# A two-layer attention kernel: which engine scales and sums q's weight in the first sample, and where the last sample's reciprocal and statistics stand

## The chip, the cores and the metric

The kernel runs on one core of one Trainium2 chip. The metric is the device time of a whole run in microseconds (us), smaller is better. Beside the plain runs there is one profiled execution, from which all the views below are taken; its times count from the start of its span.

## The reference

Eight samples of 512 channels by 1024 positions, float32, go through two attention layers one after the other. Cut to what matters:

```python
# layer 0: group norm, 8 heads of 64
h = group_norm(x, norm_w, norm_b)
q, k, v = split(einsum('oc,bchw->bohw', qkv_w, h) + qkv_b)
o = softmax(q @ k.T / sqrt(64)) @ v
x = x + einsum('oc,bchw->bohw', proj_w, o) + proj_b
# layer 1: norm over a whole sample, one head of 512
n = (x - mean) * rsqrt(var + 1e-5) * gn_gamma + gn_beta
q = wq @ n + bq;  k = wk @ n + bk;  v = wv @ n + bv
out = x + wo @ (v @ softmax(q.T @ k / sqrt(512)).T) + bo
```

In layer 1 the kernel multiplies weights together first: one 512 by 512 weight, called `wqk1` (the product of wq and wk), replaces q's and k's, and one called `wvo1` (wv and wo) replaces v's and the output's. The gain gamma is multiplied into these products, into `wqk1` by rows and by columns.

## The kernel before

**Samples and stages.** The samples are worked through one after another. Each has, in order: V of layer 0, q and k of layer 0, the attention of layer 0, the projection of layer 0 (which, for all but the last sample, comes after the next sample's first q and k), then layer 1: q, V, scores, values. What is needed only once, the two weight products and the scaling by gamma, stands ahead of the first sample and partly in it.

**Products.** Every large product is made by a fast scheme with seven block products in place of eight (`strassen`, or `by_two_steps` with the scheme inside the scheme). TensorE adds up two of a group's four results in one PSUM bank, `line`, and two in another, `single`. ScalarE copies `line` away as u1, u2 and u3 as it goes, and VectorE adds `single` and the copies together (`done`, lines 712, 729, 1285). TensorE can write `single` again only after VectorE has read it, and `line` after ScalarE has. The scheme needs sums of the weight's blocks, S1 to S4: `finish` (L195) makes them with four VectorE operations of 128x512 elements for a whole weight, and `sums_a` (L511) makes those of the second level, sixteen operations of 128x128 for one `WeightTwice`. Made once, they are stored to DRAM and read back for later samples.

**Order.** The orders on TensorE, ScalarE and VectorE are those in which the program is written. `together` takes one step of each of several products in turn, and `at_steps(steps, hooks)` runs the functions of hooks[n] after step n. GpSimd (POOL) and SyncE (SP), which issues nearly all transfers, have queues of their own, in an order that a scheduler makes at build time; each of them starts its instructions in that order. Weights stand in three buffers; a load into a buffer waits for the last reader of the weight before.

**The first sample.** The stage `pairs_qk(w, 0, ...)` makes q and k of half the channels, with ten steps. Its hooks make `wvo1` ready, run `through_q` (which multiplies rows of `wqk1` by gamma on ScalarE, L236, and its columns by a row of gamma on GpSimd, L241, eight operations of 128x256), make the second-level sums of `wvo1` on VectorE (step 5), finish the weight of V, `v0`, at step 7 and `wqk1` at step 8, and at step 9 make the second-level sums of `qk02`. The second-level sums of `wqk1` go onto a list, `over`, which the next stage, V of the first sample, takes as hooks 0 to 3; they are issued to GpSimd. `rows_q` is a transfer of a small result to DRAM, and the eight transfers `c_q` (L774) read it back in single elements of four bytes.

**The last sample.** Its projection (L1263 on, `last` true) has to divide by a sum over keys that is not there yet when it starts: four matmuls (`add_keys`, L1024) make the sum in `spares[0]`, the second half of the tile that has the first product's `single`, VectorE takes its reciprocal (L860) and multiplies. `Ready.measure` runs the next of the list `due`, each entry two passes of ScalarE over half a chunk (L333), for layer 1's mean and variance. Part way through V of layer 1, VectorE makes sums of layer 1's query, `halve_a("S1")`, at step 13.

Of the kernel before, what the change touches and what calls it, by code (L numbers as in the profile page):

```python
# [39 lines left out]
ALU = mybir.AluOpType  # L40
# [6 lines left out]
P = 128  # L47
C = 512
# [17 lines left out]
def two_attention_blocks(  # L66
# [18 lines left out]
    nc = tc.nc  # L85
# [16 lines left out]
    def tile2(name):  # L102
        return tpool.tile([P, 2, HALF], FP, tag="t", name=name)

    def tile_u(name):
        return upool.tile([P, HALF], FP, tag="u", name=name)
# [93 lines left out]
    class Weight:  # L200
# [3 lines left out]
        def __init__(self, name):  # L204
            self.name, (self.src, self.widths) = name, SOURCES[name]
            self.tile = wpool.tile([P, W_SIZE], FP, tag="w", name=f"w_{name}")
            self.parts, self.rest, at = [], [], 0
            for width in self.widths:
                size = len(A_PARTS) * 2 * width
                self.parts.append(parts_of(self.tile[:, at : at + size], width))  # L210
                at += size
            if name in stored:
                nc.sync.dma_start(self.tile, stored[name])
# [24 lines left out]
        def scale_columns(self, row):  # L238
            for cc in range(NC):
                for to, a in self.moving(cc):  # L240
                    nc.gpsimd.tensor_tensor(a, a, row[:, to], ALU.mult)  # L241

        def finish(self):
            for parts, rest in zip(self.parts, self.rest):
# [43 lines left out]
    def room(name, n=-1):  # L288

        return spares[n] if spares else banks("s", f"ps_{name}")[:, 0, :]  # L290
# [207 lines left out]
    def sums_a(q, t, engine=nc.vector):  # L498

        t = t if len(t.shape) == 2 else flat(t)  # L500
        n = t.shape[1] // 4
        for i in range(4):
            part = t[:, i * n : (i + 1) * n]
            if len(q["A11"].shape) == 3:
                part = part.rearrange("p (u o) -> p u o", u=2)
            q[f"S{i + 1}"] = part
        for i, x, y, op in [
            (1, "A21", "A22", ALU.add), (2, "S1", "A11", ALU.subtract),
            (3, "A11", "A21", ALU.subtract), (4, "A12", "S2", ALU.subtract),
        ]:  # L510
            engine.tensor_tensor(q[f"S{i}"], q[x], q[y], op)  # L511
        return q
# [36 lines left out]
    class WeightTwice:  # L549

        def __init__(self, name, make=None, later=None):
            tiles = [flat(tile2(f"{name}_twice_{n}")) for n in range(2)]
            key, self.tiles = f"{name}_twice", tiles
            if make is None:

                nc.scalar.dma_start(tiles[0], stored[key][:, : 8 * P])
                nc.scalar.dma_start(tiles[1], stored[key][:, 8 * P :])
                return  # L560
            stored[key] = dram.tile([P, 16 * P], FP, tag=key, name=f"stored_{key}")

            def step(n, i, a):
                sums_a(
                    self.quarters(a, make), tiles[n][:, i * 4 * P : (i + 1) * 4 * P],
                    nc.vector if later is None else nc.gpsimd,
                )
                if i == 1:
                    nc.sync.dma_start(stored[key][:, n * 8 * P : (n + 1) * 8 * P], tiles[n])

            steps = [
                lambda n=n, i=i, a=a: step(n, i, a)
                for n, pair in enumerate(PAIRS) for i, (a, _) in enumerate(pair)
            ]
            if later is not None:
                later.extend(steps)
                return
            for now in steps:
                now()

        def quarters(self, a, rows_of):
            return {f"A{i + 1}{j + 1}": rows_of(i, a)[:, j, :] for i in range(2) for j in range(2)}
# [275 lines left out]
    def one_over(ps, name):  # L858
        inv = accpool.tile([P, HALF], FP, tag="inv", name=f"inv_{name}")[:, : ps.shape[1]]
        nc.vector.reciprocal(inv, ps)  # L860
        return inv
# [29 lines left out]
    def both_of(w):  # L891
        return lambda i, name: w.parts[i][name]
# [34 lines left out]
    def columns_of(w):  # L927
        return lambda i, name: w.parts[0][name][:, :, i * P : (i + 1) * P]
# [26 lines left out]
    def layer0(bs, qs, ks, b, norm_next):  # L955
# [5 lines left out]
        if norm_next is not None:  # L961
            for n in range(NC):
                hooks[n + 4] = [lambda cc=n, half=half: norm_next.of_half(cc, half) for half in range(2)]
            hooks[8] = [lambda cc=cc: norm_next.of_channels(cc) for cc in range(NC)]
        for n, step in enumerate(over):
            hooks.setdefault(n, []).append(step)
        over.clear()
        twice_b = {}
        if b > 0:
# [50 lines left out]
        def add_keys(pair, gs, ps):  # L1020

            n = P // 2 // len(gs)
            for i, (g, j) in enumerate((g, j) for g in gs for j in range(2)):
                nc.tensor.matmul(  # L1024
                    ps[i * n : (i + 1) * n, :], ones[:, :n], accs[pair, g][:, j, :],
                    start=True, stop=True,
                )
# [46 lines left out]
        def combine1():  # L1074
            nc.vector.tensor_tensor(comb["T1"], os[0][1], os[0][0], ALU.subtract)
# [187 lines left out]
        def project(w, c):  # L1263
            def done(i, half, bank, u):
                chunk = c + 2 * i
                x = piece(xs, chunk, half)

                def add():
                    nc.vector.scalar_tensor_tensor(  # L1269
                        x, bank if u is None else u, bias[:, chunk : chunk + 1], x, ALU.add, ALU.add  # L1270
                    )
                    due.append(lambda: norm.moments(chunk, half, i == half))
                    if (i, half, c) == (1, 0, 1):
                        ready.halve("B21")


                first = last and i == half == 0
                if first and c == 0:
                    ps_sum = spares[0]
                    add_keys(end, [1], ps_sum)  # L1280
                    combine1()
                    combine2(2, 0)
                    combine2(3, 0)
                if u is not None:
                    nc.vector.tensor_tensor(u, bank, u, ALU.add)
                if not first:
                    add()
                    return
                later.append(add)
                if c == 0:  # L1290
                    invs[end] = one_over(ps_sum, f"0_{b}_{end}_1")
                    divide(end, 1, invs[end])
                else:

                    held(flat(accs[end, 1]), f"acc_0_{b}_{end}", flat(accs[end, 1]))
                    for n, k in [(2, 1), (3, 1), (4, 0), (4, 1)]:
                        combine2(n, k)
                    for more in later:
                        more()

            return strassen(by_channels(w, c, comb), done, f"p_0_{b}_{c}")

        w = next_weight().parts[0]
        hooks = {} if last else {2 * n - 3: [lambda n=n: combine2(n, 1)] for n in range(2, 5)}
        for n, counts in [(1, 1), (2, 1), (7, 1), (8, 2), (9, 2)]:
            hooks.setdefault(n, []).append(lambda n=counts: ready.measure(n))
        hooks[2].append(ready.load)
        hooks[7].append(lambda: ready.halve("B22"))
        at_steps(together(project(w, 0), project(w, 1)), hooks)
        if last:  # L1310
# [3 lines left out]
    class Ready:  # L1314
# [9 lines left out]
                self.due.pop(0)()  # L1324

        def load(self):
            self.weights = WeightTwice("wqk1")

        def halve(self, name, engine=nc.gpsimd):
            self.quarters[name] = quarters_b(  # L1330
# [3 lines left out]
    def attention1(xs, norm, ready, b, at_values):  # L1334
# [19 lines left out]
        def halve_a(name, t=None, engine=nc.vector):  # L1354
            q = {f"A{n}": v for n, v in halve(q_parts[name], lambda i, j: (j, i)).items()}
            twice_a[name] = sums_a(q, flat(tile2(f"{name}_twice_{b}")) if t is None else t, engine)
# [115 lines left out]
        def finish_q(n):  # L1472
            q_parts[f"S{n}"] = tile2(f"s{n}_q_{b}")
            finish(q_parts, a21, n)

        at_steps(make_v_twice(w, twice_w[0], bs, twice_b, v_pairs, f"v_1_{b}"), {
            **{2 * n + 3: [lambda n=n: finish_q(n)] for n in range(1, 5)}, 13: [lambda: halve_a("S1")],
        })


# [375 lines left out]
        nc.tensor.matmul(ps[:, 0:1], ones, good, start=True, stop=True)  # L1856
        nc.vector.tensor_copy(flag, ps[0:1, 0:1])

    made, throughs, over, gamma_row = {}, [], [], []


    with tc.manual_schedule(engines={PE, ACT, DVE}):
# [31 lines left out]
                        nc.vector.tensor_tensor(t, t, vec[:, V_NW1 : V_NW1 + NC], ALU.mult)  # L1894

        def through_v():
            gamma_row.append(tile2("gamma_row")[:, 0, :])
            nc.sync.dma_start(gamma_row[0], gamma1.to_broadcast([P, C]))
            throughs.append(Through(wvo1, bias_v, wo1, "v", room("rows_v", 0)))
            wvo1.scale_rows(V_NW1, range(1))  # L1900

        def through_q():
            throughs.append(Through(wqk1, bias_q, nk1, "q", room("rows_q", 0)))
            wqk1.scale_rows(V_NW1)
            wqk1.scale_columns(gamma_row[0])

        def channels_of(half, ccs):
            for cc in ccs:
# [21 lines left out]
        at_steps(together(*pairs_qk(w, 0, combine.parts, qs, ks, 0)), {  # L1930
            1: [lambda: combine.make(2), wvo1.finish], 2: [through_q, lambda: combine.make(3)],
            4: [lambda: combine.make(4)], 5: [lambda: WeightTwice("wvo1", columns_of(wvo1))],
            7: [waiting[0].finish], 8: [wqk1.finish], 9: [
                lambda: WeightTwice("qk02", both_of(w)), lambda: WeightTwice("wqk1", columns_of(wqk1), over),
            ],
        })
        bs = combine.parts
        for rows in throughs:
# [434 lines left out]
```

## Time and profile before

| | us | what it is |
|---|---|---|
| Median of 3 runs | 2829.9 | 2828.9 to 2829.98 |
| The profiled execution | 2828.29 | whole run |
| Its span | 2825.7 | first to last instruction |
| PE busy | 2806.3 | 99% of the span, 19.4 us idle |
| DVE (VectorE) busy | 2114.7 | 75% |
| ACT (ScalarE) busy | 1171.2 | 41% |
| POOL (GpSimd) busy | 394.3 | 14% |

A busy share is an average over stages. PE stands still for 19.4 us of the span, and the view of waits says for whom. In a timeline each line gives the start, the length, the engine, the line of the program, the operation, what it writes from what it reads, how many are merged, and in brackets the idle time before it and who ended it. "SPq" is SyncE's queue, and the length there is the time that issuing the transfer took.

### The profile page before, as it was taken

How to read it: one execution, taken by the hardware profiler on the slowest of the kernel's cores; microseconds unless marked ns; L12 is line 12 of the kernel's file. 1: busy time of each engine (PE TensorE's matmuls, PEld its weight loads, DVE VectorE, ACT ScalarE, POOL GpSimd, SP SyncE). 2: the span in 40 equal slices, each digit the busy share in tenths (PEclk: the TensorE clock that was granted, in tenths of full speed). 3: DMA queues.
4: the chain of work that ended last, by engine and by line, in shares of the span. 5: the costliest groups of instructions: out<-in, count | busy, mean ns of one | idle time of the engine just before them, and what ended most of it. 6: DMA issues, size and time to landing. Idle time of an engine off the chain costs nothing.

```text
span 2825.7 us, 39407 instructions
## 1 busy us (share of the span) xinstructions
PE 2806.3 (99%) x15688; PEld 1585.4 (56%) x15688; DVE 2114.7 (75%) x2867; ACT 1171.2 (41%) x1760; POOL 394.3 (14%) x412
## 2 busy tenths in 40 slices
PE   9999999999999999999999999999999999999999
PEld 5434765357653576435764466734667346673375
DVE  6677697776967678676787767777777777767777
ACT  3364224643246332563325533255332643326622
POOL 2000220012200231002400024000240002400121
PEclk9999999999999999999999999999999999999999
DMA  7513132231313313233131331313313132121001
GB/s 264 203 46 122 58 111 85 70 113 53 126 64 87 105 53 112 68 91 109 70 106 45 91 124 56 108 49 87 121 57 108 50 114 93 64 95 48 23 16 39
DMA packets 83865, 247.50 MB, mean 88 GB/s; under 512 B 21817, under 2 KB 22617, under 8 KB 77273
## 3 DMA queue, kind: packets, MB, share of 16 engines
q1 hardware_dynamic: 73768, 209.75, 22.6%
q10 hardware_dynamic: 9904, 35.16, 3.8%
q8 instruction: 125, 2.05, 0.3%
q14 instruction: 68, 0.55, 0.1%
HBM read 188.02 MB, written 33.03 MB: 78 GB/s over the span
## 4 chain that ended last, share of the span: by engine, by line
PE 92%; DVE 6%; issue 1%; DMA 0%; ACT 0%; ACTq 0%; POOL 0%; DVEq 0%; POOLq 0%
PE s L992 16%; PE ps_o L1011 16%; PE ps_o L1686 7%; PE ps_v L695 7%; PE ps_p L680 6%; PE ps_l_qk L917 5%; PE ps_l L1522 4%; PE ps_s L1505 4%; PE ps_s_qk L910 4%; PE ps_l_q L680 3%; PE ps_l_v L695 3%; PE ps_s L1522 3%; PE ps_o_qk L910 3%; PE ps_s_v L938 2%; PE ps_s_q L1380 2%; PE ps_s_two L1816 2%
## 5 line engine op out<-in xcount | busy, mean ns | idle before, releaser
L846 ACT ACTIVATE p<-s 128x1024 f32<-128x1024 f32 x512 | 523.5, 1024 | 329.2 <-PE s L992 323.1
L848 DVE TENSOR_TENSOR acc<-acc,p 128x1024 f32<-128x1024 f32 x384 | 469.1, 1222 | 99.2 <-ACT p L846 90.3
L1011 PE MATMUL ps_o<-p,v 64*64 64x512 f32 x4096 | 528.7, 589 | 0.0
L992 PE MATMUL s<-c_q,c_k 64*64 64x512 f32 x3584 | 465.1, 590 | 0.0
L1011 PEld LDWEIGHTS ps_o<-p,v 64*64 64x64 f32 x4096 | 156.6, 133 | 282.8 <-issue 278.0
L992 PEld LDWEIGHTS s<-c_q,c_k 64*64 64x64 f32 x3584 | 134.7, 133 | 253.2 <-issue 236.1
L528 POOL TENSOR_TENSOR B_twice<-x 128x512 f32<-128x512 f32 x16 | 20.4, 1274 | 1353.8 <-DVE x L1269 1353.3
L1686 PE MATMUL ps_o<-t_p,s_v 128*128 128x512 f32 x384 | 168.2, 594 | 0.0
L848 DVE TENSOR_TENSOR acc<-p,p 128x1024 f32<-128x1024 f32 x64 | 78.2, 1222 | 79.7 <-ACT p L846 79.7
L1496 ACT ACTIVATE p<-p,factor 128x512 f32<-128x512 f32 (+1 forms) x112 | 85.3, 780 | 115.9 <-DVE p L1532 91.4
L1510 ACT COPY p<-ps_s 128x512 f32<-128x512 f32 x96 | 53.1, 588 | 176.6 <-PE ps_s L1505 176.6
L1686 PEld LDWEIGHTS ps_o<-t_p,s_v 128*128 128x128 f32 x384 | 72.3, 190 | 91.3 <-issue 89.2
L1532 DVE TENSOR_TENSOR p<-ps_l,p 128x512 f32<-128x512 f32 x136 | 89.8, 682 | 40.0 <-PE ps_l L1522 39.7
L459 ACT COPY u_v<-ps_v 128x512 f32<-128x512 f32 x48 | 28.1, 585 | 212.3 <-PE ps_v L695 193.4
L680 PE MATMUL ps_p<-t_p,w_p 128*128 128x512 f32 x256 | 112.8, 593 | 1.8 <-ACT u_p L459 1.2
L1532 DVE TENSOR_TENSOR p<-ps_s,p 128x512 f32<-128x512 f32 x112 | 74.8, 684 | 37.8 <-PE ps_s L1522 37.8
L695 PE MATMUL ps_v<-w_v,t_again 128*128 128x256 f32 x448 | 99.0, 379 | 0.0
L373 POOL TENSOR_TENSOR rstd<-rstd,minus_half 128x4 f32<-128x4 f32 (+1 forms) x16 | 12.8, 798 | 567.3 <-DVE rstd L372 567.3
L695 PEld LDWEIGHTS ps_v<-w_v,t_again 128*128 128x128 f32 x448 | 85.1, 190 | 11.6
L695 PE MATMUL ps_v<-w_v,x 128*128 128x256 f32 x384 | 87.3, 380 | 0.9 <-DVE q L712 0.9
L680 PE MATMUL ps_p<-o,w_p 128*128 128x512 f32 x192 | 86.9, 594 | 0.2 <-DVE o L1031 0.2
L680 PEld LDWEIGHTS ps_p<-t_p,w_p 128*128 128x128 f32 x256 | 48.5, 190 | 63.7 <-issue 59.1
(507 smaller groups left out, 5165.8 us busy)
## 6 DMA issues: line engine op xcount, KB each, us to landing
x<-in_x SPq DMA_DIRECT2D x92, 512.0 KB, 6.5
w_qk<-stored_qk SPq DMA_DIRECT2D x14, 1792.0 KB, 7.2
w_wqk<-stored_wqk SPq DMA_DIRECT2D x8, 1792.0 KB, 7.2
fold<-acc SPq DMA_DIRECT2D x56, 256.0 KB, 3.1
qk_twice<-stored_qk_twice ACTq DMA_DIRECT2D x28, 512.0 KB, 5.9
w_wvo<-stored_wvo SPq DMA_DIRECT2D x8, 1792.0 KB, 8.8
out<-x SPq DMA_DIRECT2D x28, 512.0 KB, 4.8
w_v<-stored_v SPq DMA_DIRECT2D x7, 1792.0 KB, 7.4
```

Of the source, the lines that this page charges most:

```text
L680: nc.tensor.matmul(bank, w[a][:, k, c * P : (c + 1) * P], bs[b][:, k, :], start=fresh and k == 0, stop=k == 1, skip_group_check=True,)
L695: nc.tensor.matmul(bank[:, u * 2 * P : (u + 1) * 2 * P], bs[b][:, k, n * P : (n + 1) * P], w[a][:, k, :], start=fresh and u == k == 0, sto ...
L846: nc.scalar.activation(p, s, AF.Exp, scale=factor)
L848: nc.vector.tensor_tensor(acc, first, p, ALU.add)
L910: nc.tensor.matmul(bank[:, i * 2 * P : (i + 1) * 2 * P], parts[a][x], twice_b[v][y], start=start and i == 0, stop=True, skip_group_check=True,
L917: nc.tensor.matmul(bank, of(i, a)[:, k, :], bs[v][:, k, :], start=start and k == 0, stop=k == 1, skip_group_check=True,)
L992: nc.tensor.matmul(s[cols, j, :], ks[pair][k0 // HALF][rows, k0 % HALF : k0 % HALF + HD], qs[pair][g][rows, :], start=True, stop=True,)
L1011: nc.tensor.matmul(o[cols, half, :], vs[kt][rows, c0 : c0 + HD], p[rows, j, :], start=kt == 0, stop=kt == NT - 1,)
L1505: nc.tensor.matmul(bank, bs[v][:, k, t * P : (t + 1) * P], q_parts[a][:, k, :], start=a == "A11" and k == 0, stop=k == 1, skip_group_check ...
L1522: nc.tensor.matmul(bank[:, u * 2 * P : (u + 1) * 2 * P], v[y][:, u * P : (u + 1) * P], a[x], start=start and u == 0, stop=True, skip_group ...
L1532: nc.vector.tensor_tensor(at(r, t), bank, at(r, t), ALU.add)
L1686: nc.tensor.matmul(bank, v_parts[kt // 2][a][:, kt % 2, c * P : (c + 1) * P], p_parts[kt // 2][b][:, kt % 2, cols], start=fresh and kt == ...
```

## The change

In the first sample the multiplication of `wqk1`'s columns by gamma goes from GpSimd to VectorE, out of `through_q` and into step 2 of V; `wqk1.finish` goes from step 8 of the stage before to step 3 of V; `v0`'s finish goes from step 7 to step 8, behind VectorE's add for q there. The second-level sums of `wqk1` go from GpSimd, in V, to VectorE, at step 5 of the first sample's projection, where the kernel before read them back from DRAM. The row of gamma is loaded after `rows_q` is stored and not before the first sample.

In the last sample ScalarE copies the sum over keys to a tile `total`, and the reciprocal reads that; the first two `measure` go from steps 1 and 2 to steps 5 and 6; `halve_a("S1")` goes from step 13 to 17.

```diff
@@ scale_columns
-                    nc.gpsimd.tensor_tensor(a, a, row[:, to], ALU.mult)
+                    nc.vector.tensor_tensor(a, a, row[:, to], ALU.mult)
@@ WeightTwice.__init__(self, name, make=None)
-            def step(n, i, a):
-                sums_a(
-                    self.quarters(a, make), tiles[n][:, i * 4 * P : (i + 1) * 4 * P],
-                    nc.vector if later is None else nc.gpsimd,
-                )
...
-            if later is not None:
-                later.extend(steps)
-                return
...
+            for n, pair in enumerate(PAIRS):
+                for i, (a, _) in enumerate(pair):
+                    sums_a(self.quarters(a, make), tiles[n][:, i * 4 * P : (i + 1) * 4 * P])
+            for n in range(2):
+                nc.sync.dma_start(stored[key][:, n * 8 * P : (n + 1) * 8 * P], tiles[n])
@@ layer0
-        for n, step in enumerate(over):
-            hooks.setdefault(n, []).append(step)
+        for n, step in over:
+            hooks.setdefault(n, []).insert(0, step)
@@ the projection
                 if first and c == 0:
-                    ps_sum = spares[0]
+                    ps_sum, total = spares[0], tile_u(f"total_0_{b}")
                     add_keys(end, [1], ps_sum)
+                    nc.scalar.copy(total, ps_sum)
...
-                    invs[end] = one_over(ps_sum, f"0_{b}_{end}_1")
+                    invs[end] = one_over(total, f"0_{b}_{end}_1")
...
-        for n, counts in [(1, 1), (2, 1), (7, 1), (8, 2), (9, 2)]:
+        for n, counts in [(5, 1), (6, 1)] if last else [(1, 1), (2, 1)]:
             hooks.setdefault(n, []).append(lambda n=counts: ready.measure(n))
-        hooks[2].append(ready.load)
+        for n, counts in [(7, 1), (8, 2), (9, 2)]:
+            hooks.setdefault(n, []).append(lambda n=counts: ready.measure(n))
+        hooks.setdefault(2 if b else 5, []).append(ready.load)
@@ Ready.load
-            self.weights = WeightTwice("wqk1")
+            self.weights = WeightTwice("wqk1", None if self.b else columns_of(waiting[0]))
@@ V of layer 1
-            **{2 * n + 3: [lambda n=n: finish_q(n)] for n in range(1, 5)}, 13: [lambda: halve_a("S1")],
+            **{2 * n + 3: [lambda n=n: finish_q(n)] for n in range(1, 5)}, 17 if last else 13: [lambda: halve_a("S1")],
@@ ahead of the first sample
         def through_v():
-            gamma_row.append(tile2("gamma_row")[:, 0, :])
-            nc.sync.dma_start(gamma_row[0], gamma1.to_broadcast([P, C]))
             throughs.append(Through(wvo1, bias_v, wo1, "v", room("rows_v", 0)))
...
         def through_q():
             throughs.append(Through(wqk1, bias_q, nk1, "q", room("rows_q", 0)))
+            gamma_row = tile2("gamma_row")[:, 0, :]
+            nc.sync.dma_start(gamma_row, gamma1.to_broadcast([P, C]))
             wqk1.scale_rows(V_NW1)
-            wqk1.scale_columns(gamma_row[0])
+            over.extend([(2, lambda: wqk1.scale_columns(gamma_row)), (3, wqk1.finish)])
...
-            7: [waiting[0].finish], 8: [wqk1.finish], 9: [
-                lambda: WeightTwice("qk02", both_of(w)), lambda: WeightTwice("wqk1", columns_of(wqk1), over),
-            ],
+            8: [waiting[0].finish], 9: [lambda: WeightTwice("qk02", both_of(w))],
```

## The prediction

> **What bounds the kernel now.** I read the shares first: PE is busy for 2806.3 of 2825.7 us, so only its 19.4 us of idle time can be won by edits that change no product. The waits of PE say where that time lies:
>
> ```profile
> PE ps_v L695 <- DVE v L729: 4.3, 1, 4.3
> PE ps_l_v L695 <- DVE c_v L631: 1.9, 1, 1.9
> PE ps_q L680 <- DVE q L712: 1.8, 1, 1.8
> ...
> PE ps_p L680 <- ACT u_p L459: 1.2, 1, 1.2
> ...
> PE ps_v L695 <- DVE q L712: 0.9, 1, 0.9
> PE ps_p L680 <- DVE inv L860: 0.6, 1, 0.6
> ```
>
> Each occurs once. The timeline puts the two for q and that for v in the first sample (57.2, 65.2, 75.2 us), those for u_p, inv and c_v in the last (2668.4, 2660.1, 2720.2). These are the places that the change edits. Before 57 us VectorE is late; its timeline shows why:
>
> ```profile
> 52.30 0.70 DVE L511 TENSOR_TENSOR wvo_twice<-wvo_twice,w_wvo 128x128 f32<-128x128 f32 x1
> 52.92 0.81 DVE L511 TENSOR_TENSOR wvo_twice<-w_wvo 128x128 f32<-128x128 f32 x1
> ...
> 55.97 0.28 DVE L511 TENSOR_TENSOR wvo_twice<-w_wvo 128x128 f32<-128x128 f32 x1
> 56.17 0.28 DVE L511 TENSOR_TENSOR wvo_twice<-w_wvo,wvo_twice 128x128 f32<-128x128 f32 x1
> ```
>
> The same operation takes 0.70 to 0.81 us while GpSimd runs the scaling (L241, 46.0 to 53.6 us) and 0.28 once GpSimd is idle. The weight of V can't be loaded before these sums have read its buffer. SP's timeline:
>
> ```profile
> 46.27 0.38 SPq L766 DMA_DIRECT2D rows_q<-row_q  x1
> 54.22 0.32 SPq L569 DMA_DIRECT2D stored_wvo_twice<-wvo_twice  x1
> 56.48 0.33 SPq L220 DMA_DIRECT2D w_v<-in_s_v  x1
> 56.87 0.42 SPq L569 DMA_DIRECT2D stored_wvo_twice<-wvo_twice  x1
> 57.38 6.04 SPq L774 DMA_DIRECT2D c_q<-rows_q  x6
> ```
>
> The load goes out at 56.48, as the last sum ends, and lands at 61.7; v0's sums, wqk1's (65.0 to 68.1) and qk02's (68.8 to 74.5) follow on VectorE, and then the add that PE waits for at 75.18. The chain of waits agrees: from 41.4 to 74.5 us it is VectorE's, but for that load. Behind that wait PE is slow as well, as the busy times by window show (stretch, its length, PE busy and count, clock, DMA share, GB/s):
>
> ```profile
> 71.00:74.00 3.00, 0.00 (x0) 1.00 0.90 382
> ...
> 75.20:77.00 1.80, 1.80 (x4) 0.50 0.67 133
> 77.00:79.00 2.00, 2.00 (x8) 0.68 0.87 286
> 79.00:81.00 2.00, 2.00 (x11) 1.00 1.04 424
> ```
>
> The ten products from 75.18 to 94.07 take 18.9 us and not 10 x 1.72 = 17.2: 1.7 us go to the half clock.
>
> **What the Trainium skill says.** "GPSIMD Engine Reference", section "1. Specifications", has GpSimd share SBUF interfaces with VectorE, with contention for VectorE instructions with two SBUF inputs; the trace agrees (0.28 against 0.70 to 0.81). "SBUF — State Buffer", section "SBUF: two separate sides", calls that an exclusive lock, held for an instruction, and says that transfers and engines don't contend there; with GpSimd idle and transfers running at 55 to 56 us the sums take 0.28, which agrees. "DMA: Bandwidth & Descriptors", section "Anatomy of one DMA — SWDGE (gpsimd) path", says that a wait for a semaphore happens on the issuing sequencer before dispatch: what stands behind a waiting transfer on SP's queue waits too. The trace agrees: w_v goes out when its wait ends, and c_q only behind it. "TensorE: Matmul & The Clock Gate", section "Part 1: The HAM clock gate (the "warmup" mystery)", halves TensorE's clock after an idle window of about 3.4 us. The trace agrees: half behind 4.3 us of idleness here, full behind each of the waits of 1.8 to 1.9 us.
>
> **First sample, part by part.** Steps between starts are shorter than durations, so I use them: 0.22 us for an undisturbed 128x128 sum (55.04 to 56.37 has six in 1.33), 0.34 for 128x256, 0.61 for 128x512, 1.715 for four 512-wide matmuls.
>
> *VectorE up to the load.* The eight scalings leave GpSimd. Then t (46.85) takes 1.15 in place of 1.68 and the sixteen sums of wvo1 16 x 0.22 = 3.5 in place of 7.84: they end at 51.5 and not at 56.4. The adds for q and k follow ScalarE's copies (52.6, 54.3), and PE's product at 57.17 starts at 55.23 (53.51 + 1.715): 1.94 won. Three more products bring PE to V at 60.4, before 62.4.
>
> *The load of v0's weight.* It isn't earlier by 5 us, since the change alters SP's queue: ahead of it now stand the row of gamma, five c_q, the first store of wvo1's sums and one more c_q. The first c_q must wait for rows_q to land, 46.27 + 7.4 = 53.7, behind the store of wvo1. Each c_q takes SP 0.55 in a quiet stretch (c_v: seven in 3.85) and 1.0 in a busy one (six in 6.04 above). With 0.55 the load goes out at 53.7 + 6 x 0.55 + 0.35 = 57.35; with 1.0 at 60.1. I take the quiet figure and a little more, 57.7, since transfers are idle from 52.3 us on. Landing took 5.3; the 512 KB store just ahead should cost a little more, the six c_q no longer behind it a little less: 63.1. Both ends: 62.6 and 66.
>
> *From the load to v.* PE idles from 60.4 to 63.1. VectorE, from there: v0's sums 2.5, k's add 0.65, sixteen sums of qk02 3.5, v's add 0.65: 70.4. PE has 32 matmuls of 0.215 (6.9) before it needs v: 70.0. So PE goes on at 70.5 in place of 75.18: **4.7 us won**; 5.2 and 1.8 at the ends. And its longest pause is 2.7 us in place of 4.3, short of the window, so the clock stays: **1.7 won**. This is lost again if the load lands much behind 63.8 (60.4 + 3.4). wqk1's finish is no longer ahead of v, nor GpSimd's sixteen sums beside qk02's (5.7 us became 3.5).
>
> *What is late next.* Behind v's two adds VectorE has the scaling (8 x 0.34 = 2.7), wqk1's finish (4 x 0.61 = 2.4) and four statistics (2.5): from 71.0 to 78.6. Its next add for PE is due near 79.9 (behind six of PE's products and a copy; before: at 86.25, after 8.15 us of idleness). It is covered, with 1.3 to spare; without that cover PE would wait at the fourth pair of products, up to the excess. wqk1's store goes out at 77 and qk02's reload behind it; the projection's weight is issued at V's end as before, and is needed 15 us later.
>
> *The sixteen sums in the first projection.* VectorE idles there for 5.85 us (265.4 to 271.3), and GpSimd until 274.6: 16 x 0.22 = 3.5 fits, cost nothing. If each took 0.54 as beside GpSimd, 8.6, PE would lose up to 2.8. Two transfers leave ScalarE's queue and two stores join SP's behind wvo1's load and ahead of v0's (279.25): nothing waits for them soon.
>
> **Last sample.** *Copy and reciprocal.* S1 of the first product starts at 2660.08, 0.9 later than 2655.76 + 3.43 = 2659.19, as the reciprocal (2656.68, 3.34 us) reads the tile it writes. With the copy it can start at 2659.19. But VectorE's order stays: the add ahead of the reciprocal now waits for the copy (ScalarE 2655.93 to 2656.5, so the add ends 0.45 later), the reciprocal still takes 3.35 (no row shows 512 columns read from SBUF; the 32-wide one, 344 ns, is no faster per column; I take no gain, a gain of 1 us would end here), and behind it stand a multiply and the add that frees the second product's bank: 2661.8. S1 of the second product starts at 2661.9, and before at 2661.8. **Nothing won.**
>
> *Statistics behind copies.* S3 starts at 2668.37, 1.4 late, as ScalarE makes two statistics ahead of the u2 copies. Now the copies come first, and S3 starts at 2661.9 + 3 x 1.715 = 2667.0: 1.35 won. The statistics are moved behind, though: ScalarE (1.6 each, held up between u3 copies) reaches the third at about 2672.0 in place of 2672.59, so GpSimd's chain from 2682.8 on, for the mean, comes 0.6 to 0.7 earlier while PE comes 1.35 earlier. That chain's last instruction ends at 2689.44 and PE's averaging matmul starts at 2689.39, so there is no slack to pay with. **0.8 won.** Bounds: 0.6 and 1.35.
>
> *halve_a at step 17.* In samples before the last, PE takes 3.57 us from the first line product to the next (314.88 to 318.45); in the last 5.57 (2714.66 to 2720.23), as GpSimd makes its sums beside VectorE's and slows them (0.83 to 0.94 against 0.42), and L631 stands behind them. Moved past, it isn't behind them: **2.1 won**. The four sums, some 1.4 us at 2722.4, then delay the last L631 by 0.3; their first reader is 10 us on. Bounds 1.5 and 2.1.
>
> **Sum.** 4.7 + 1.7 + 0.8 + 2.1 = 9.3 us: against the profiled execution 2828.3 - 9.3 = 2819.0. The median of the runs shown is 1.6 above that execution, so a median should be 2820.6.
>
> **Rivals.** *The load of v0's weight comes late.* With c_q at 1.0 us it lands at 66, and PE idles 5.6 us, so the clock falls too: 1.8 + 0 + 2.9 = 4.7, 2825.2. For it: c_q had a median of 1.02 us here; against it: the queue is quiet at 53.7. *The last sample gives nothing*: GpSimd's or ScalarE's chain holds PE fully and halve_a only moves the stall on: 6.4, 2823.5. Against it: seven samples go through the same stage with no such wait. *Slower: c_q holds SP's queue.* The longest c_q took 2.18 us. VectorE, and so PE, is late by whatever the load is late: all gains are gone when PE goes on at 78.1, so the load lands at 70.7 and leaves at 65.4: c_q at 1.9 each. At 2.9 each it leaves at 71.5, PE goes on at 84.2, and the time is 2836. For it: 512 elements of four bytes per transfer, six of them ahead; against it: c_v's seven took 0.37 to 0.68. *The change does not do what it says*: VectorE is slowed by its own small operations and not by GpSimd. Then wvo1's sums still end at 56.4, the load leaves at 57.4, qk02's sums take 5.7, and PE goes on at 72.6: 2.6 + 1.7 + 2.9 = 7.2, 2822.7. The 0.28 us rows speak against it.
>
> **How the numbers follow.** About 0.2% (5.7 us) is what a measurement of this kernel can tell from no change. The main case, 2820.6 (its own range 2818.5 to 2823), has 0.66; the late load 0.15, the last sample giving nothing 0.08, sums slow in themselves 0.04, the blocked queue 0.07. Faster by over 0.2% are 0.64 of the main case, 0.03 of the late load (its near end), 0.06 and 0.04 of the next two: 0.77. Slower is 0.04 of the blocked queue; same the rest, 0.19. The range for 8 in 10 goes from the main case with every bound at its good end (10.4, and a run near the profiled one's time) to just beyond the late load: 2818 to 2826.5.
>
> **What would show it.** Right: wvo1's sums at 0.28 us each ending near 51.5, w_v issued at 57 to 58 behind six c_q, PE's wait for w_v near 2.7 us, no wait over 0.8 for v L729, a clock of 1.00 all through V, no wait for c_v L631 or inv L860 in the last sample, a new short one at the averaging matmul. Wrong: c_q over 1 us each and w_v landing after 66; a wait in the first projection behind the sixteen sums; a wait for the add behind the statistics near 80 us.

## The result, and the profile after

The changed kernel takes 2820.0 us (median of 7 runs, 2818.54 to 2821.61) against 2829.98 us (7 runs, 2828.9 to 2830.52): a ratio of 0.9965, 95% interval 0.9953 to 0.9977. Its profiled execution took 2819.71 us with a span of 2818.0 us; before it was 2828.29 and 2825.7. The spans differ by 7.7 us, the profiled executions by 8.6, the medians by 10.0. Of the 2.3 us between the first and the last of these, 0.9 lie outside the span, from the first to the last instruction: a whole run is longer than its span by 2.63 us in the kernel before (median of the 43 runs timed beside `first_only`) and by 1.75 in the changed one. Most of the rest is chance: the profiled execution of the kernel before was a quick one, with 2825.7 us where the spans of those 43 runs have a median of 2826.8.

The waits of PE in the changed kernel (what waited, for what: us in total, times, longest):

```profile
PE ps_v L682 <- DMA w_v<-in_s_v: 3.4, 1, 3.4
PE ps_l L1512 <- DVE p L1522: 1.2, 7, 0.2
PE ps_warm L1859 <- POOL in_sample L164: 1.2, 1, 1.2
PE ps_p L667 <- DVE u_p L1273: 0.6, 1, 0.6
```

All six waits at the places of the change are gone: v, both q, u_p (for ScalarE's copy), inv and c_v. In their place stand one of 3.4 us for the load of v0's weight in the first sample, and in the last one of 0.6 us for the add behind the reciprocal; it stands ahead of S1 of the second product, where the old wait for inv stood ahead of S1 of the first. (The other two, L1512 and the warming, were there before.) SP's timeline (start, duration, queue, line, transfer, count) shows why the load is awaited:

```profile
46.39 0.38 SPq L753 DMA_DIRECT2D rows_q<-row_q  x1
46.82 0.91 SPq L1893 DMA_DIRECT2D gamma_row<-in_gamma  x1
53.38 2.57 SPq L761 DMA_DIRECT2D c_q<-rows_q  x5
56.05 0.46 SPq L566 DMA_DIRECT2D stored_wvo_twice<-wvo_twice  x1
56.55 0.43 SPq L761 DMA_DIRECT2D c_q<-rows_q  x1
57.09 0.85 SPq L220 DMA_DIRECT2D w_v<-in_s_v  x1
```

VectorE's timeline shows the last sum that reads the buffer, the first sum that waits for the load, and the add that PE needs for S1, the next product of V:

```profile
51.62 0.28 DVE L511 TENSOR_TENSOR wvo_twice<-w_wvo,wvo_twice 128x128 f32<-128x128 f32 x1
...
64.01 0.69 DVE L195 TENSOR_TENSOR w_v<-rest_v,w_v 128x512 f32<-128x512 f32 x1 [6.01 <-DMA w_v<-in_s_v]
...
70.94 0.68 DVE L716 TENSOR_TENSOR v<-ps_v,u_v 128x512 f32<-128x512 f32 x1
```

The last sum has read the buffer at 51.9 us. The store of `wvo1` (`stored_wvo`, out at 45.97) reads the same buffer and has landed at 52.8. The load goes out at 57.1, behind six c_q, the first of which waits until `rows_q` has landed at 53.4. It lands at 64.0; v is added at 71.62, but PE comes to S1 only at 72.69. The busy times by window say what keeps it (stretch, length, busy us and count of PE, weight load, VectorE, ScalarE, GpSimd, then clock, DMA share, GB/s):

```profile
60.00:64.00 4.00, 0.65 (x2) 0.01 (x1) 0.00 (x0) 0.00 (x0) 0.00 (x0) 1.00 0.90 285
64.00:65.00 1.00, 0.97 (x4) 0.92 (x5) 0.95 (x2) 0.00 (x0) 0.00 (x0) 0.91 0.52 92
65.00:66.00 1.00, 1.00 (x4) 0.73 (x3) 1.00 (x3) 0.00 (x0) 0.00 (x0) 0.50 0.04 0
...
67.00:68.00 1.00, 1.00 (x3) 0.81 (x3) 0.97 (x5) 0.59 (x1) 0.00 (x0) 0.50 0.54 229
68.00:69.00 1.00, 1.00 (x5) 0.85 (x4) 0.96 (x6) 0.00 (x0) 0.00 (x0) 0.88 1.09 459
```

Behind the idle 3.38 us the clock goes to half, and the 32 matmuls of 256 columns that come before S1 ("the 32 products" from here on) take 8.66 us (64.03 to 72.69) and not 6.9. So the half clock has moved from behind the wait for v to behind the wait for w_v.

Where PE stood at the same product, before against after, places the gain. V ends at 94.07 against 89.96 us: 4.1. At the last sample's second pair of o's products (2655.76 against 2651.38) it is 4.4; some 0.3 came in small pieces between. S3 of the projection: 5.8. The averaging matmul: 5.6. S1 in the next stage (2720.23 against 2712.50): 7.7.

### The profile page after: what moved, and what is told of

Its sections match the earlier page's. It is cut to its first block, busy times and chain, and to the rows that moved or that the text cites. A ratio compares the mean times of both kernels' runs of the same rounds, so it can differ in the third digit from the quotient of the medians.

```text
span 2818.0 us, 39402 instructions
## 1 busy us (share of the span) xinstructions
PE 2805.0 (100%) x15688; PEld 1586.0 (56%) x15688; DVE 2113.7 (75%) x2891; ACT 1172.3 (42%) x1761; POOL 377.7 (13%) x388
## 4 chain that ended last, share of the span: by engine, by line
PE 92%; DVE 6%; issue 1%; DMA 1%; SPq 0%; ACT 0%; POOL 0%; DVEq 0%; ACTq 0%; POOLq 0%
PE s L979 15%; PE ps_o L998 15%; PE ps_v L682 7%; PE ps_o L1676 7%; PE ps_p L667 7%; PE ps_l_qk L904 5%; PE ps_l L1512 4%; PE ps_s L1495 4%; PE ps_s_qk L897 4%; PE ps_l_v L682 3%; PE ps_l_q L667 3%; PE ps_s L1512 3%; PE ps_o_qk L897 3%; PE ps_s_v L925 2%; PE ps_s_q L1370 2%; PE ps_s_two L1806 2%
## 5 line engine op out<-in xcount | busy, mean ns | idle before, releaser
L459 ACT COPY u_v<-ps_v 128x512 f32<-128x512 f32 x48 | 28.1, 586 | 210.1 <-PE ps_v L682 191.2
```

## The experiments

Each was timed beside the kernel before, whose median was 2829.5 to 2830.0 us in these comparisons.

**Half of the change each.** `first_only` takes the three edits of the last sample back:

```diff
-                    ps_sum, total = spares[0], tile_u(f"total_0_{b}")
+                    ps_sum = spares[0]
-                    nc.scalar.copy(total, ps_sum)
-                    invs[end] = one_over(total, f"0_{b}_{end}_1")
+                    invs[end] = one_over(ps_sum, f"0_{b}_{end}_1")
-        for n, counts in [(5, 1), (6, 1)] if last else [(1, 1), (2, 1)]:
+        for n, counts in [(1, 1), (2, 1)]:
-            ..., 17 if last else 13: [lambda: halve_a("S1")],
+            ..., 13: [lambda: halve_a("S1")],
```

> The change without its three edits of the last sample (the reciprocal reads PSUM, the statistics stand ahead of the copies, S1 is halved at step 13). My theory, that the traces' milestones add up: the first sample gives 4.1 us (V ends at 90.0 us as with the whole change), some 0.3 us comes by drift, and the last sample's waits are back: for u_p about 1.2, for c_v about 1.9 us. So 2829.98 - 4.4 = 2825.6 us, ratio 0.9984 (0.9979 to 0.9990). Rival, that the drop of 10.0 us between the medians, larger than the 7.7 us between the spans, lies in the first sample: then this has about 2823.3 us, ratio 0.9976 or less.

Measured: 2824.09 us, ratio 0.9982 (0.9975 to 0.9988); span 2821.1. The waits for inv (0.6), u_p (1.2) and c_v (1.9) are back and V ends at 90.07.

`last_only` makes the same edits, the other way round, in the kernel before.

> The kernel before with the three edits of the last sample alone; q's weight is scaled and summed beside GpSimd as before. My theory: the first sample is as before (wait for v of 4.3 us, half clock behind it), and the last gives 0.0 (copy of the total) + 1.25 (statistics) + 2.1 (halving) = 3.35 us: 2826.6 us, ratio 0.9988 (0.9983 to 0.9993). Rival, that the last sample's gain needs the first sample's (other times of arrival of transfers): under 1.5 us, ratio 0.9995 or more.

Measured: 2825.15 us, ratio 0.9985 (0.9979 to 0.9992); span 2822.5. S1 of the last sample's v follows without a wait. By median the halves give 5.4 and 4.4 us, together 9.8 against 10.0 for the whole; by span 4.6 and 3.2, together 7.8 against 7.7. The halves add up, and neither needs the other. Both medians lie 1.5 us below what I expected, as I had taken the halves from the spans of profiled executions, of which that of the kernel before was a quick one, and set them against a median.

**The load of v0's weight and c_q.** `columns_half` leaves four c_q on SP and sends the other four from ScalarE's queue near the end of V; `columns_later` sends all eight from there; `columns_early` sends them as V begins. The edit of `columns_early`:

```diff
         for rows in throughs:
-            rows.fetch()
+        throughs[0].fetch()
...
+        if b == 0:
+            throughs[1].fetch(nc.scalar, 0)
+            hooks.setdefault(0, []).append(lambda: throughs[1].fetch(nc.scalar, 1))
```

(`fetch` gets a queue and the number of the vector; in `columns_later` both calls are hooks, at steps 7 and 8 of V, and in `columns_half` the second alone is, at step 7.)

> The change, but four of the eight c_q (those of the second vector) go out late in V from ScalarE's queue, so SP has four and not six ahead of the load of v0's weight. My theory: the load goes out about 1.0 us earlier (56.0 to 56.1 us), lands at 62.9 and PE idles 2.3 us in place of 3.4; that is too short for the clock to fall, so the 32 products ahead of v take 6.9 us and not 8.7, and PE goes on at S1 when VectorE has added v, near 70.5 us in place of 72.69: 2.2 us less than the change, 2817.8 us. Rival, that the clock falls at every start of V whatever the idle time: the half clock stays, S1 at 71.6, 1.1 us less. Rival, that SP's order doesn't hold the load: it goes out at 57.1 as before and nothing changes.

Measured: 2818.7 us, ratio 0.9962 (0.9949 to 0.9976). This run's first sample stood 1.2 us earlier from the start (rows_q at 45.18 us). That is chance: six kernels with the same code up to there send rows_q at 45.06 to 46.54 us in their traces. So I compare within the run. The load goes out 10.1 us behind rows_q and not 10.7; PE idles 2.69 us and not 3.38. But the 32 products take 8.63 us:

```profile
59.00:62.00 3.00, 0.44 (x2) 0.00 (x0) 0.00 (x0) 0.00 (x0) 0.00 (x0) 1.00 0.80 324
62.00:63.00 1.00, 0.87 (x2) 0.81 (x3) 0.85 (x2) 0.00 (x0) 0.00 (x0) 0.53 0.57 229
63.00:64.00 1.00, 1.00 (x4) 0.73 (x4) 1.00 (x2) 0.00 (x0) 0.00 (x0) 0.50 0.06 16
...
65.00:66.00 1.00, 1.00 (x5) 0.85 (x4) 0.96 (x4) 0.22 (x1) 0.00 (x0) 0.76 0.54 229
```

A miss: 2.69 us of idleness is enough for the half clock. From rows_q to V's end this kernel is 0.7 us quicker than the changed one; the medians differ by 1.3, and their intervals overlap.

> The change, but all eight c_q go out late in V from ScalarE's queue. My theory: the load of v0's weight goes out when its first reader has ended, near 52.5 us, and lands near 58.5, before PE wants it (60.65): no wait for w_v, clock 1.00 all through, S1 at 67.5 us in place of 72.69: 5.2 us less than the change, 2814.8 us, ratio to before 0.9946. Rival, that another thing than c_q holds the load (the store of wvo1's sums, transfers in flight): it goes out after 56 us and the gain is under 2 us. Rival, that VectorE holds PE next: a wait for v or for the scaling behind it, S1 after 69 us, gain under 3.7.

Measured: 2821.09 us, ratio 0.9972 (0.9960 to 0.9983). V went as expected: load out at 52.37, no wait, 32 products in 6.9 us, V's end at 84.38. Then the gain was given back, since the columns came too late for their own reader. PE's largest wait is

```profile
PE ps_q L667 <- DVE q L699: 4.5, 1, 4.5
```

and in VectorE's timeline the reader of c_q holds the queue ahead of that add:

```profile
91.74 0.17 DVE L770 TENSOR_TENSOR c_q<-c_q 128x8 f32<-128x8 f32 x1 [4.24 <-DMA c_q<-rows_q]
```

The clock was at half for 6.8 us behind it.

> The change, but all eight c_q go out from ScalarE's queue as V begins (four ahead of its first copy, four behind it), so that they are neither ahead of v0's load nor late for q. My theory: the load goes out at 52.4 us and lands near 59, no wait for w_v, clock 1.00 through V, S1 at 67.1 and V's end at 84.4 us, as where they went out late; and no wait for q behind V, since c_q land near 66 us, some 19 us ahead of their first reader at 85 us. 5.6 us less than the change: 2814.4 us, ratio to before about 0.9948. Rival, that the four transfers ahead of ScalarE's first copy (4 x 0.5 us) hold the copies and with them PE: a wait of up to 2 us early in V, 2816.5 us. Rival, that PE's next limit is VectorE's scaling and statistics behind v: a wait near 75 us.

Measured: 2814.22 us, ratio 0.9945 (0.9931 to 0.9958): 5.8 us below the changed kernel, and the best version here. PE's timeline goes from k to V without a pause:

```profile
59.35 7.07 PE L682 MATMUL ps_v<-w_v,x 128*128 128x256 f32 x32
66.26 9.01 PE L682 MATMUL ps_v<-w_v,t 128*128 128x256 f32 x41
```

From PE's arrival at V to V's end it takes 24.2 us, against 29.3 in the changed kernel and 31.7 before. ScalarE's first copy waited for the four transfers ahead of it without PE noticing. The load went out at 51.88 us, 1.1 behind the last sum: SP waited 2.6 us for the store of `wvo1` to land. So that store is what holds the load next.

**Does the idle time make the clock fall?** `kept_warm` puts ten extra products, whose result is overwritten, where PE would be idle; `warm_short` puts three:

```diff
+            if (name, n2, a) == ("v_0_0", 0, "A11"):
+                for n in range(10):
+                    nc.tensor.matmul(bank, in_sample, bs["B11"][:, 0, :], start=True, stop=True)
             multiply(bank, a, b, fresh)
```

> The change, with ten products of 512 columns, whose result is overwritten, at the head of V, where PE would be idle from 60.65 to 64.03 us: they end near 62.8 and leave 1.2 us of idleness. My theory, that the half clock of V's first products comes from the idle time: the clock stays at 1.00, the 32 products ahead of v take 6.9 us in place of 8.7, and PE goes on at S1 when v is added, at 71.6 us in place of 72.69: 1.0 us less, 2819.0 us. Rival, that the low clock has another cause (the first products with a weight that has just landed, the transfers beside them): the 32 products still take 8.7 us and nothing is won.

Measured: 2822.14 us, ratio 0.9974 (0.9964 to 0.9983). The time was a miss by my own count: each product stands as two records of 0.43 us, so ten took 8.6 us (60.17 to 68.75) and ended 4.7 us behind the load. The clock answer holds: 1.00 throughout, and the 32 products took 6.9 us.

> The change with three extra products at the head of V in place of ten: in the run with ten each took 0.86 us (two records of 0.43), and not 0.21 as I had counted, so that they ended 4.7 us after the load had landed and cost 3 us. Three take 2.6 us and end near 63.2 us, 0.8 us ahead of the load. My theory: the clock stays at 1.00 (it did with ten), the 32 products ahead of v take 6.9 us, and PE goes on at S1 when v is added, near 71.6 us in place of 72.69: 2819.0 us, 1.0 us less than the change. Rival, that 0.8 us of idleness and a fresh weight are enough for the low clock: 8.7 us again, nothing won.

Measured: 2819.95 us, ratio 0.9966 (0.9954 to 0.9979). The clock stays at 1.00, the 32 products end with 0.57 us of PE waiting for v, and from PE's arrival at V to its end it takes 28.1 us in place of 29.3. So the trace has the microsecond at its place; the median, 2819.95 against 2820.0, does not show it. That execution also had small waits for o elsewhere, 0.8 and 0.6 us in total, which the changed kernel's had not.

**Is it GpSimd that slows VectorE?** `busy_beside` is `columns_early` with GpSimd working where it did before:

```diff
             wqk1.scale_rows(V_NW1)
+            for cc in range(NC):
+                for to, a in wqk1.moving(cc):
+                    nc.gpsimd.tensor_tensor(both[:, 1, to], a, a, ALU.mult)
```

> The kernel with the eight c_q from ScalarE's queue as V begins (2814.2 us), and beside it eight products of 128x256 on GpSimd into a spare half of gamma's tile, where the kernel before scaled q's weight; nothing waits for them, they are extra work. My theory, that GpSimd's work slows VectorE's: wvo1's sums take 0.6 to 0.8 us while GpSimd is busy and end 4 us later, near 55 us; PE waits for q, the load of v0's weight goes out 4 us later, and PE goes on at S1 3 to 4 us later, 2817.5 to 2818.5 us. Rival, that the sums of the kernel before were slow by themselves or by what they waited for: they stay at 0.28 us, nothing moves, 2814.2 us.

Measured: 2814.67 us, ratio 0.9947 (0.9930 to 0.9964). The mechanism is shown, in VectorE's timeline on both sides of GpSimd's end at 51.6 us:

```profile
50.51 0.58 DVE L511 TENSOR_TENSOR wvo_twice<-wvo_twice,w_wvo 128x128 f32<-128x128 f32 x1
51.02 0.70 DVE L511 TENSOR_TENSOR wvo_twice<-w_wvo 128x128 f32<-128x128 f32 x1
51.64 0.28 DVE L511 TENSOR_TENSOR wvo_twice<-w_wvo,wvo_twice 128x128 f32<-128x128 f32 x1
```

The price was a miss: the sums end 3.0 us later (53.8 against 50.8) and the load goes out 1.9 us later (53.80 against 51.88), but it lands only 0.75 later and V ends 0.5 us later. Of the 3.0 us, 1.1 don't count because the load of `columns_early` waits for the store of `wvo1` and not for the sums, and 1.2 are gone because the load lands in 5.2 us here and in 6.4 there, which no run explains. What is left costs V half a microsecond.

`scaled_in_place` changes one word of the kernel before, `nc.gpsimd` to `nc.vector` in `scale_columns`.

> The kernel before with one line changed: q's weight scaled by VectorE where it stands, ahead of wvo1's sums, and not moved into V. wqk1's second sums stay on GpSimd. My theory: VectorE has 8 x 0.34 = 2.7 us more and loses the slowing by GpSimd (4.9 us), so wvo1's sums end near 54.1 us and not at 56.4, the load goes out 2.3 us earlier, and v is added 2.3 us earlier: 2827.4 us, ratio 0.9992 (0.9985 to 0.9997), with a wait for v of 4 us or more and the half clock behind it still there. Rival, that moving the scaling out of this stretch is what counts and the slowing is small: no gain or a loss, 2829.5 to 2832 us.

Measured: 2827.85 us, ratio 0.9994 (0.9986 to 1.0003): not told apart from no change. wvo1's sums run at 0.28 us, but the products t ahead of them wait for the scaling and are slowed by GpSimd's first sums (1.48 us in place of 1.22), so the load goes out 9.7 us behind rows_q against 10.2 before. The wait for v is 4.3 us as before.

**What the deferral is worth.** `not_deferred` is `columns_early` with the scaling and wqk1's finish at their old places, on VectorE:

```diff
-            over.extend([(2, lambda: wqk1.scale_columns(gamma_row)), (3, wqk1.finish)])
+            wqk1.scale_columns(gamma_row)
...
-            8: [waiting[0].finish], 9: [lambda: WeightTwice("qk02", both_of(w))],
+            7: [waiting[0].finish], 8: [wqk1.finish], 9: [lambda: WeightTwice("qk02", both_of(w))],
```

> The kernel with the eight c_q from ScalarE's queue (2814.2 us), but q's weight is scaled by VectorE ahead of wvo1's sums and finished ahead of v, where the kernel before had these steps; v0's sums stand at step 7 again. Only the sixteen second sums stay in the first projection, so GpSimd is idle here, and no c_q is ahead of the load. My theory, that most of the first sample's gain is VectorE's work taken out from before v: 2.7 us of scaling ahead of the load, 2.4 us of sums behind it; v is added near 70.4 us and not 65.8, PE waits about 3 us for it, and the clock falls behind that wait (1.7 us more): V ends 4 to 6 us later, 2818.3 to 2820.1 us. Rival, that GpSimd's slowing was the cost and VectorE has room for these steps: under 1.5 us more, below 2815.7 us.

Measured: 2825.98 us, ratio 0.9987 (0.9980 to 0.9993), well beyond my range, for a reason that I had not seen. The load of gamma's row now goes out at 45.8 us, with the step, and the scaling in VectorE's queue waits for it:

```profile
53.00 0.43 DVE L241 TENSOR_TENSOR w_wqk<-w_wqk,gamma_row 128x256 f32<-128x256 f32 x1 [8.07 <-DMA gamma_row<-in_gamma]
```

PE waited 7.7 us for t behind it. So the late load of gamma's row is possible only because the scaling is deferred. What stands behind the load of w_v can still be read. From the first of v0's sums to v added it takes 13.3 us in the kernel before (61.84 to 75.13), 10.8 here (67.07 to 77.87) and 7.6 in the changed kernel (64.01 to 71.62). GpSimd's silence is worth 2.5 us there, wqk1's finish and q's add out of the way 3.2.

**The last sample's edits.** `no_copy` and `early_statistics` each take one edit back, as in the first diff.

> The change with the reciprocal of the total read from PSUM again. My theory: the wait for the reciprocal comes back as 0.6 us ahead of S1 of the first product, and the wait for u_p ahead of the second product (0.65 us) goes: PE comes to the second product at the same time within 0.1 us. 2820.0 us. Rival, that the copy is worth what its wait was: 0.6 to 0.9 us more, 2820.8 us, and the wait for u_p stays.

Measured: 2819.37 us, ratio 0.9965 (0.9952 to 0.9979). The wait for inv is back (0.5 us), the one for u_p gone, and PE reaches the second product 5.91 us after the second pair of o's products began, against 6.07 with the copy. The copy wins nothing.

> The change with the last sample's first two statistics ahead of ScalarE's copies again. My theory: S3 of the last sample's projection waits for u_p again, 1.15 to 1.4 us, and the first line product of the next stage is 1.25 us later against the clock of the run: 2821.2 us. Rival, as in the prediction, that GpSimd's chain for the mean limits PE: then it comes with that chain, and only 0.6 to 0.8 us is lost.

Measured: 2821.39 us, ratio 0.9970 (0.9959 to 0.9981). The wait for u_p is back with 1.54 us, and the averaging matmul stands 27.98 us behind the second product's start in place of 26.33: 1.65 us by the trace, 1.4 by the medians, whose intervals overlap.

## Why the prediction was right, and where not

The forecast was 2820.6 us and the measured 2820.0. That closeness is partly luck: the steps gave 9.3 us and their counterparts in the trace 7.7. Two errors that have nothing to do with the steps made up for it. I had put nothing outside the span, where 0.9 us were won, and I had added 1.6 us for the median over the profiled execution, where the changed kernel's median lies 0.3 above.

*VectorE up to the load*: right. The sums take 0.28 us, end at 51.9 (said 51.5), and PE reaches V at 60.65 (60.4). Left out was the store of `wvo1`, which reads the buffer until 52.8: with SP's queue free the load could have gone out then, and not at 51.9.

*The load of v0's weight*: the order of SP's queue and its price were right. Issue at 57.1 (57.7), c_q at 0.5 us each. Mis-sized was the landing: from the issue to VectorE's first sum 6.9 us and not 5.4, so 64.0 and not 63.1. With c_q just ahead it took 6.4 to 7.3 us in seven kernels, without them 5.2 and 5.3 (`busy_beside`, `not_deferred`) but also 6.4 and 6.8 (`columns_early`, `columns_later`). So c_q alone don't explain it, and what adds the microsecond stays open.

*From the load to v*: this is the step that failed. "Short of the window, so the clock stays: 1.7 won" is wrong twice. The pause was 3.38 and not 2.7 us; and `columns_half` shows that 2.69 us also brings the half clock. I had read the window as a stretch of idleness that must be 3.4 us long. "TensorE: Matmul & The Clock Gate", section "Part 1: The HAM clock gate (the "warmup" mystery)", calls the window free-running, which is another thing, and the runs agree with that (below). The old half clock behind v did go, 1.6 us (the ten products from S1 take 17.27 in place of 18.9), but a new one came ahead of S1. S1 was won by 2.5 us and not 4.7: v's add came 1.2 later than said (the landing), PE another 1.07 behind it (the clock). The first sample gave 4.1 and not 6.4 us.

The load is also not where the gain came from, though I had begun there. It landed 2.2 us later than before (64.01 against 61.84). The gain is in the 5.7 us less of VectorE's time between the load and v, which `not_deferred` splits. That GpSimd slows VectorE is shown. Ahead of the load that slowing cost little where it was tried, 0.5 us in `busy_beside`; in the kernel before, with its other order of transfers, it wasn't tried alone.

*What is late next* and *the sixteen sums*: right. No wait near 80 us; the sums run from 261.25 to 265.06 in VectorE's pause.

*Copy and reciprocal*: right, nothing won, by the step named: the reciprocal, the multiply and the add still stand in that order. *Statistics*: counted from the start of the second product, 1.26 us by the trace at the averaging matmul, where I took 0.8 of 0.6 to 1.35. At S3 1.42 was won; of it 0.15 went back at 2681.09, where PE now waits for the add of c_q behind t on VectorE, and none went to GpSimd's chain as I had thought. *halve_a*: 2.1, right.

*The rivals*: the late load came half true, since its landing was late and the clock fell, though c_q took 0.5 us each and not 1.0. The blocked queue did not happen, but `columns_early` shows that c_q's place cost 5.8 us by the medians, 5.1 of them between PE's arrival at V and V's end.

## What to carry to other kernels

Before crediting an engine's relief, see what stands beside it at the same gate: here the buffer was free 4 us before the load could go, because small transfers had moved ahead of it in the issuing queue. When small transfers are moved, find their own reader first: too early they held the load, too late they held q, and of the places tried only V's start cost nothing that PE's waits show. A pause of PE is paid twice, by its length and by the half clock behind it, so a wait that is shortened to under 3 us may still cost the clock.

## What the runs showed that I had not expected

The clock does not answer to the length of a pause alone. In quarter-microsecond windows:

| kernel | PE idle, us | length | clock falls | rises |
|---|---|---|---|---|
| before, wait for c_v | 2718.3 to 2720.2 | 1.95 | not | |
| columns_half | 59.44 to 62.13 | 2.69 | 62.1 | 65.5 |
| early_statistics | 59.33 to 62.58 | 3.25 | 62.1 | 65.6 |
| first_only | 60.80 to 64.13 | 3.33 | 65.2 | 68.6 |
| the change | 60.65 to 64.03 | 3.38 | 64.8 | 68.2 |
| no_copy | 59.50 to 63.03 | 3.53 | 62.7 | 66.1 |
| before | 70.88 to 75.18 | 4.30 | 74.9 | 78.3 |
| last_only | 70.19 to 74.50 | 4.31 | 73.4 | 80.2 |
| scaled_in_place | 69.96 to 74.27 | 4.31 | 73.3 | 80.1 |
| columns_later | 91.41 to 95.94 | 4.53 | 95.1 | 101.9 |
| not_deferred | 49.38 to 57.06 | 7.68 | 52.6 | 62.8 |

It falls 2.6 to 4.4 us after the pause begins, in two runs 0.8 and 1.1 us after work has resumed, and stays at half for 3.4, 6.8 or 10.2 us. That fits fixed stretches of 3.4 us, each judged by how much work it held. Those that ended in a fall held up to 1.1 us of work; any such stretch around the pause of 1.95 us held at least 1.5. The half clock was left where the next stretch had up to 0.4 us of idleness, and kept where it had 0.9 us or more (`columns_later`, `last_only`, `scaled_in_place`, and two stretches in `not_deferred`). With that, pauses of the same 4.3 us cost 1.6 us in the kernel before, 2.9 in `last_only` and 3.0 in `scaled_in_place`. The reading fits all eleven rows; no run varied the pause alone to prove it.

The 0.9 us outside the span go with one word. A run is longer than its span by 2.63 us in the kernel before and by 2.55 in `last_only`, but by 1.75 in `scaled_in_place`, where only the engine of the scaling differs, and by 1.7 to 1.8 in every other kernel here. It isn't GpSimd's multiplying as such, since `busy_beside` has 1.78. The cause stays open.

GpSimd is slowed as well: in `busy_beside` its product of 128x256 took 1.37 and 1.59 us beside VectorE's t of 128x1024 and 0.66 beside the small sums.
